# Three edits in a two-model chain of local-attention layers: where the root's steps lie, how far ahead one model projects, and the loop order of a product

## The chip, the cores and the metric

The kernel runs on one core of a Trainium2 chip. The core has five engines that run side by side, each through its own list of instructions in order: TensorE (PE; its weight loads are listed as PEld), VectorE (DVE), ScalarE (ACT), GpSimd (POOL) and SyncE (SP), which here issues the DMAs. They wait for one another through semaphores. Matrix products land in PSUM, which PE writes and DVE and ACT read; the tiles of all other data lie in SBUF. The metric is the device time of one execution in microseconds (us), lower is better.

## The reference, cut to what matters

Two models follow each other on an input of shape (2, 2048, 128). Each is modulated, attends, and then runs a chain of local-attention layers:

- first model: an attention stage, then 6 layers with 16 heads of 64, windows of 32
- second model: a linear-attention stage, then 2 layers with 8 heads of 64, windows of 64

The part that the change touches is inside the local-attention layers. For each layer:

```
def l2norm(t):
    return t / jnp.clip(jnp.linalg.norm(t, axis=-1, keepdims=True), 1e-12)
...
q, k, v = jnp.split(h @ wqkv, 3, axis=-1)
q = l2norm(q) * qs
k = l2norm(k) * ksc
q, k = rotary_xpos(q, k)
o = local_attention(q, k, v)     # softmax over the window before and the own window
x = x + o @ wo
h = layernorm(shift_token(x)) @ w1 + b1
x = x + (a * gelu(g)) @ w2 + b2  # a, g: the halves of h
```

Everything is float32. The root of the title is the reciprocal square root of the sum of squares of every head of queries and keys, that is, l2norm.

## The kernel before, in words

The first model's attention stage runs up to about 600 us of the span and is not touched. Then `local_models` runs all 8 layers as one list of 256 tiles: layer by layer, 16 tiles of 128 tokens for each of the 2 sequences, the two sequences taking turns. Tiles 0 to 191 are the first model's, 192 to 255 the second's.

A loop over rounds i (L1461) works on several tiles at once. In round i:

- `scores(i + 1)`: on PE a mask (L986) and the products of queries and keys (L995) into a wide buffer; DVE takes the maximum (L1003) and subtracts it (L1005). Then ACT takes the exponential (L1012), DVE sums (L1019) and inverts (L1020), and POOL multiplies (L1021).
- `project(i + 3, ...)`, once for each unit of the model (the first model has two units, for its 2048 columns of queries and keys, the second has one): two products (L871) into a wide buffer `pq`; ACT squares it (L873); DVE multiplies it by the cosine table into `r` (L881) and, with the halves swapped, by the sine table into `t2` (L886); POOL adds the two (L892). After the last unit DVE sums the squares of each head (L897), takes the root in `rsqrt_quick` (L167 to L180, nine small instructions), and POOL multiplies `r` by it (L904).
- `keys_first_(i)`: the weights of tile i are transposed (L1030) and copied by ACT (L1031).
- `mix(i)`: the value product (L1048), copied by ACT (L1054).
- `values(i + 2)`: the value projection (L955), copied by ACT (L956) and spread to windows by SP's DMAs (L963 to L968).
- `turn(i + 2, u)`: `r` is transposed (L936) and copied to query and key tiles by ACT (L939, L941). Tile i + 2 was projected in round i - 1.
- `project_out(i)`: the output product (L1065), added to the residual by DVE (L1071).

Between these calls a round takes two steps (`step`) from a list of feed-forward work and up to six (`lstep`) from a list of the second model's linear-attention work. `feed_forward` adds seven steps after every fourth tile of a sequence: centring (L1096), variance (L1105, L1108, L1110), a pause, scaling (L1128, L1131), two times three products (L1148) with ACT (L1158) or DVE (L1165) behind, and a last product (L1173, L1179). The linear-attention steps run while the first model's last layer ends and the second's first layer starts. A tile of the second model whose input isn't complete forces further steps (`while (b, t // 4) not in ready`).

PSUM has eight banks of 512 float32 in each partition. `wide` gives out two buffers of two banks (pool `f_psA`) and `bank` four buffers of one bank (pool `f_psT`):

```
psA = ctx2.enter_context(tc.tile_pool(name="f_psA", bufs=2, space=PSUM))
psT = ctx2.enter_context(tc.tile_pool(name="f_psT", bufs=4, space=PSUM))
```

The scores and the projections take wide buffers, and so do some of the linear-attention steps; all other products take single banks. In the kernel before, L897 and the root's steps write into `pq`, the wide buffer of the last unit, once the product in it has been used:

```
y = rsqrt_quick([pq[:, k * 32:k * 32 + 2 * H] for k in range(4)], 2 * H, wk)
```

A wide buffer is free when the last reader of what it holds is done. The first model takes three of them in a round (scores, unit 0, unit 1), so the next round's unit 0 gets the buffer of this round's unit 1.

The framework (tile pools) inserts the waits, and it plans the order of the instructions of each engine from the traced program, its own estimate of durations and the buffers that are free then. So the order on an engine is near that of the source, but not the same: in the trace the first records of a value product (L1048) often stand ahead of a value projection (L955), and the rest of the product behind it.

In `mix` the value product is cut into many small products. For the first model each works on 64 of the 128 rows (the key group s) and 64 of the 128 columns (the half q): four quarters of PE's array, each with weights of 64 x 64 and 32 columns of data. The second model has one key group (NO is 1), so each takes all rows and one half of the columns. Every float32 product stands in the trace as two records.

## Time and profile before

| | us |
|---|---|
| median of 3 runs (4983.2 to 4993.75) | 4991.75 |
| the profiled execution | 4992.08 |
| its span (first to last instruction) | 4990.3 |
| PE busy in the span | 4522.4 |
| DVE busy | 3949.9 |
| POOL busy | 2783.4 |
| ACT busy | 2641.9 |

The profile is that of one execution. Its page gives busy time of each engine and the busy share in 40 slices of the span, each of them 125 us. Groups of instructions are named by line, engine, operation and tile names (written <- read). A row of the waits names the instruction that an idle engine was waiting to start and what it waited for; a PE wait is time that PE is idle. PEclk is the clock that PE was granted, 1.00 being full speed. In the timeline each row has the start in us from the span's start, the length in us, the engine, the line, what was done and how often (x), and in square brackets the idle time of the engine before it. PE's matmuls overlap each other, so the length of a group of them includes the tail of the last one.

The stages that the text speaks of: the first model's layers from 600 to 3700 us, the change of models with its linear attention from 3700 to 4300, the rest of the second model from 4300 on.

### The profile page before, as it was taken

What the parts mean: (1) busy time and instruction counts of PE and PEld (TensorE: products, weight loads), DVE (VectorE), ACT (ScalarE), POOL (GpSimd) and SP (SyncE); (2) the same over time, 40 slices, a digit from 0 to 9 for tenths busy, and PEclk for the clock granted to TensorE, in tenths of its full rate; (3) what the DMA queues carried; (4) which work ended last, traced back from release to release, by engine and by line L of the source; (5) the groups of instructions that cost most, each with busy time, mean ns of one, the idle gap of its engine ahead of it and who ended that gap; (6) DMA issues with size and microseconds to landing.
All of it is one profiled execution on the core that took longest, in us unless ns stands there. A gap on an engine that the chain in (4) does not pass through costs nothing.

```text
span 4990.3 us, 166474 instructions
## 1 busy us (share of the span) xinstructions
PE 4522.4 (91%) x73028; PEld 3080.9 (62%) x73058; DVE 3949.9 (79%) x6840; ACT 2641.9 (53%) x4207; POOL 2783.4 (56%) x1666
## 2 busy tenths in 40 slices
PE   5667799999999999999999999999999998989887
PEld 3445566666666666666666666666666665555554
DVE  6993488888887888888888888888877777778776
ACT  3223355555555555555555555555555555555554
POOL 3332366666666666666666666666555544455552
PEclk8778899999999999999999999999999999999999
DMA  2000222223222322232222322232221211111111
GB/s 77 1 1 25 84 68 67 64 72 78 68 64 63 84 71 64 64 82 72 65 70 61 80 67 64 66 82 68 55 58 49 63 45 40 40 46 40 50 48 41
DMA packets 222468, 295.32 MB, mean 59 GB/s; under 512 B 75656, under 2 KB 95408, under 8 KB 221744
## 3 DMA queue, kind: packets, MB, share of 16 engines
q1 hardware_dynamic: 221744, 284.67, 22.1%
q8 instruction: 576, 9.44, 0.8%
q14 instruction: 148, 1.21, 0.1%
HBM read 40.98 MB, written 10.75 MB: 10 GB/s over the span
## 4 chain that ended last, share of the span: by engine, by line
PE 47%; DVE 25%; ACT 7%; POOL 6%; issue 4%; DMA 1%; SPq 0%; POOLq 0%; DVEq 0%; ACTq 0%
PE ps_qk L871 11%; PE ps_o L1048 5%; PE ps_f L1148 5%; DVE ps_qk L897 5%; PE ps_v L955 5%; DVE t L886 5%; PE ps_turn L936 4%; POOL r L892 4%; PE ps_y L1065 4%; PE ps_s L995 3%; DVE r L881 3%; PE ps_fy L1173 3%; DVE rs L1019 2%; ACT sq L873 2%; PE ps_pT L1030 2%
## 5 line engine op out<-in xcount | busy, mean ns | idle before, releaser
L892 POOL TENSOR_TENSOR r<-r,t 128x1024 f32<-128x1024 f32 x448 | 1061.8, 2370 | 926.2 <-DVE t L886 814.6
L904 POOL TENSOR_TENSOR r<-r,rq_y 128x1024 f32<-128x1024 f32 x448 | 844.5, 1903 | 521.8 <-DVE rq_y L180 498.9
L873 ACT ACTIVATE sq<-ps_qk 128x1024 f32<-128x1024 f32 x448 | 461.0, 1029 | 1091.5 <-PE ps_qk L871 1026.4
L871 PE MATMUL ps_qk<-wp,hs 128*128 128x512 f32 x1792 | 894.9, 622 | 110.0 <-DVE rq_y L180 82.6
L881 DVE TENSOR_TENSOR r<-ps_qk,tb 128x1024 f32<-128x1024 f32 (+1 forms) x512 | 550.9, 1076 | 215.2 <-ACT sq L873 200.9
L1048 PEld LDWEIGHTS ps_o<-pT,v 64*64 64x64 f32 (+1 forms) x26624 | 479.4, 136 | 309.5 <-ACT pT L1031 162.4
L886 DVE TENSOR_TENSOR t<-ps_qk,tb 128x1024 f32<-128x1024 f32 (+1 forms) x512 | 554.5, 1083 | 145.5 <-POOL r L892 145.0
L1021 POOL TENSOR_TENSOR sm<-sm,rs 128x1024 f32<-128x1024 f32 x256 | 487.9, 1906 | 255.5 <-DVE rs L1020 172.7
L1048 PE MATMUL ps_o<-pT,v 64*64 64x32 f32 (+1 forms) x26624 | 532.1, 221 | 36.5 <-ACT pT L1031 19.9
L897 DVE TENSOR_REDUCE ps_qk<-sq 128x16 f32<-128x1024 f32 x448 | 549.2, 1226 | 12.0
L871 PEld LDWEIGHTS ps_qk<-wp,hs 128*128 128x128 f32 x1792 | 310.5, 193 | 367.6 <-issue 236.5
L936 PEld LDWEIGHTS ps_turn<-ident,r 128*128 128x128 f32 x3584 | 413.1, 144 | 157.0 <-issue 98.2
L936 PE MATMUL ps_turn<-ident,r 128*128 128x128 f32 x3584 | 450.1, 278 | 40.4 <-POOL r L904 36.9
L955 PE MATMUL ps_v<-wp,hs 128*128 128x512 f32 x896 | 482.2, 640 | 1.1 <-ACT oT L1054 0.8
L1065 PEld LDWEIGHTS ps_y<-oT,wo 128*128 128x128 f32 x3584 | 432.1, 193 | 48.3 <-issue 43.0
L1065 PE MATMUL ps_y<-oT,wo 128*128 128x128 f32 x3584 | 448.5, 277 | 1.7 <-ACT oT L1054 1.5
L1003 DVE TENSOR_REDUCE mx<-ps_s 128x16 f32<-128x1024 f32 (+1 forms) x256 | 312.5, 1221 | 101.5 <-PE ps_s L995 99.6
L1054 ACT COPY oT<-ps_o 128x512 f32<-128x512 f32 x448 | 243.8, 588 | 276.0 <-PE ps_o L1048 275.2
L995 PE MATMUL ps_s<-kT,qT 64*32 64x64 f32 (+1 forms) x26624 | 384.1, 231 | 0.3 <-issue 0.3
L995 PEld LDWEIGHTS ps_s<-kT,qT 64*32 64x32 f32 (+1 forms) x26624 | 331.0, 108 | 63.1 <-issue 49.4
L1148 PE MATMUL ps_f<-fx,w 128*128 128x512 f32 (+1 forms) x768 | 364.5, 612 | 2.3 <-DVE fx L1131 1.9
L1019 DVE TENSOR_REDUCE rs<-sm 128x16 f32<-128x1024 f32 (+1 forms) x256 | 310.6, 1213 | 62.3 <-ACT sm L1012 61.2
(265 smaller groups left out, 6860.3 us busy)
## 6 DMA issues: line engine op xcount, KB each, us to landing
v<-vn SPq DMA_DIRECT2D x1276, 128.0 KB
v<-vn SPq DMA_DIRECT2D x744, 64.0 KB
v<-vn SPq DMA_DIRECT2D x64, 256.0 KB
wp<-in_L_ffn_Wqkv SPq DMA_DIRECT2D x20, 512.0 KB
xD<-xb SPq DMA_DIRECT2D x24, 256.0 KB
xb<-xD SPq DMA_DIRECT2D x24, 256.0 KB
cs<-in_cos SPq DMA_DIRECT2D x128, 32.0 KB
cs<-in_sin SPq DMA_DIRECT2D x128, 32.0 KB
```

Of the source, the lines that this page charges most:

```text
L871: nc.tensor.matmul(pq[:, js], lhsT=hw, rhs=wts[g, u][:, js], start=True, stop=True)
L881: nc.vector.tensor_tensor(r[:, es].rearrange("p (h d) -> p h d", d=DH), pq[:, es].rearrange("p (h d) -> p h d", d=DH), bc(tb[:, 0, s].unsq ...
L886: nc.vector.tensor_tensor(t2[:, es].rearrange("p (h s d) -> p h s d", s=2, d=32), pq[:, es].rearrange("p (h s d) -> p h s d", s=2, d=32)[: ...
L892: nc.gpsimd.tensor_tensor(r, r, t2, ALU.add)
L897: nc.vector.tensor_reduce(pq[:, 16 * v:16 * v + 16], st[i].pop(("sq", v)).rearrange("p (h d) -> p h d", d=DH), AX.X, ALU.add,)
L904: nc.gpsimd.tensor_tensor(rv, rv, bc(y[:, 16 * v:16 * v + 16].unsqueeze(2), (128, 16, DH)), ALU.mult)
L936: nc.tensor.transpose(p[:, c * 128:(c + 1) * 128], r[:, cs], ident)
L955: nc.tensor.matmul(p, lhsT=hw, rhs=wv, start=True, stop=True)
L995: nc.tensor.matmul(sp[W * w:W * w + W, c0:c0 + 2 * W], lhsT=qT[64 * q:64 * q + 64, cc, W * w:W * w + W], rhs=kT[64 * q:64 * q + 64, cc, W ...
L1048: nc.tensor.matmul(po[s][64 * q:64 * q + 64, 128 * c + W * w:128 * c + W * w + W], lhsT=v2[kp, w, co:co + 64], rhs=pT[kp, q, c, W * w:W * ...
L1065: nc.tensor.matmul(py[:, 0:128], lhsT=wts[g, "o"][:, c * NO + s, :], rhs=oT[:, s, c, :], start=(c + s == 0), stop=(c == 3 and s == NO - 1),)
L1148: nc.tensor.matmul(ps_[c][0:sz], lhsT=wts[g, "w1"][:, o:o + sz], rhs=S["x"], start=True, stop=True,)
```

## The change

It has three parts. First, L897 and the root's steps write into a single bank `ss` of the pool of four, instead of into the wide buffer `pq`. Second, a tile of the second model is projected four rounds ahead instead of three: a table `rounds` says which tiles are projected in a round, and since tile 191 is projected in round 188 and tile 192 too, that round has both. The second model's `r` takes turns between the two tags that the first model has for its two units, so that it has four buffers. Third, in `mix` the loop over the key group s (row halves) becomes the outer and the loop over q (column halves) the inner one of the two.

```diff
-            r = wk.tile([128, 1024], F32, name=f"r{u}", bufs=2)
+            r = wk.tile(
+                [128, 1024], F32, tag=f"r{u if len(units) == 2 else i % 2}", name="r", bufs=2
+            )
...
+                ss = bank("ss")
                 for v in range(len(units)):
                     nc.vector.tensor_reduce(
-                        pq[:, 16 * v:16 * v + 16],
+                        ss[:, 16 * v:16 * v + 16],
                         st[i].pop(("sq", v)).rearrange("p (h d) -> p h d", d=DH), AX.X, ALU.add,
                     )
-                y = rsqrt_quick([pq[:, k * 32:k * 32 + 2 * H] for k in range(4)], 2 * H, wk)
+                y = rsqrt_quick([ss[:, k * 32:k * 32 + 2 * H] for k in range(4)], 2 * H, wk)
...
                 for w in range(m.NW):
-                    for q in range(2):
-                        co = 128 * c + 64 * q
-                        for s in range(NO):
-                            kp = slice(2 * W * s, 2 * W * (s + 1))
+                    for s in range(NO):
+                        kp = slice(2 * W * s, 2 * W * (s + 1))
+                        for q in range(2):
+                            co = 128 * c + 64 * q
                             nc.tensor.matmul(
...
+        rounds = {}
+        for j in range(n):
+            rounds.setdefault(j - (3 if len(layers[tiles[j][0]][0].units) == 2 else 4), []).append(j)
         for i in range(-3, n):
-            j = i + 3
             lstep()
...
-            more = False
-            if j < n:
+            for j in rounds.get(i, ()):
                 g, b, t = tiles[j]
...
-                lstep()
+            lstep()
             step()
...
-            if j < n:
+            for j in rounds.get(i, ()):
+                g, b, t = tiles[j]
+                jj = j % per
+                nu = len(layers[g][0].units)
+                more = g < last
                 project(j, nu - 1)
```

## The prediction, made before the change was run

> **What bounds the kernel now.** I read the busy shares first, then the same shares by stage, then TensorE's waits in each stage, and last one wait in the timeline. All sums are made against the profiled execution: 4992.1 us, of which its span is 4990.3 and 1.8 lies around it. The median of the runs shown is 4991.75, so both stand for the same time. A measurement of this kernel can tell about 0.2% (10 us) from no change.

> The page, engines over the whole span and in 40 slices:
> ```profile
> PE 4522.4 (91%) x73028; PEld 3080.9 (62%) x73058; DVE 3949.9 (79%) x6840; ACT 2641.9 (53%) x4207; POOL 2783.4 (56%) x1666
> ...
> PE   5667799999999999999999999999999998989887
> ...
> DVE  6993488888887888888888888888877777778776
> ```
> TensorE (PE) is busy 9 tenths or more from slice 7 on; VectorE (DVE) never is. By stage (first model, change of models, second model; the columns are the stretch, its length, busy PE, PEld, DVE, ACT, POOL, then the granted PE clock):
> ```profile
> 600.00:3700.00 3100.00, 2977.08 (x56700) 2048.85 (x56700) 2583.03 (x4180) 1769.10 (x2778) 1986.25 (x1156) 0.99 0.28 69
> 3700.00:4300.00 600.00, 556.42 (x6820) 372.74 (x6820) 446.92 (x870) 329.02 (x501) 294.73 (x192) 0.96 0.18 49
> 4300.00:4990.30 690.30, 594.69 (x5113) 377.37 (x5108) 516.72 (x1077) 350.28 (x527) 321.40 (x200) 0.94 0.16 45
> ```
> PE is 96% busy in the first model and DVE 83%: PE sets the pace, and only PE's own idle time (123 us there) and its clock can be won. In the second model PE is 86% busy and idle 96 us. What ends those idle times, first stage and then last stage (waiter, releaser: us in all, times, longest):
> ```profile
> PE ps_qk L871 <- DVE rq_y L180: 82.3, 80, 3.7
> PE ps_o L1048 <- issue: 14.4, 19, 1.8
> PE ps_qk L871 <- DVE sm L1005: 8.8, 16, 3.4
> ```
> ```profile
> PE ps_turn L936 <- POOL r L904: 32.8, 11, 3.5
> PE ps_out L1439 <- DVE xb L1195: 13.2, 4, 4.6
> PE ps_o L1048 <- ACT pT L1031: 10.0, 28, 0.7
> PE ps_r L1128 <- POOL frt L1110: 6.6, 2, 4.3
> PE ps_qk L871 <- DVE sm L1005: 6.0, 11, 0.8
> PE ps_s L986 <- DVE rq_y L180: 5.0, 5, 2.0
> ```
> The first line is the wide buffer. The last unit's product holds it until the root's last step (L180); the second wide buffer after it is the next round's first product (L871). One such wait:
> ```profile
> 2525.84 1.23 DVE L886 TENSOR_TENSOR t<-ps_qk,tb 128x1024 f32<-128x1024 f32 x1 [1.30 <-POOL r L892]
> ...
> 2533.28 0.19 DVE L180 SCALAR_TENSOR_TENSOR rq_y<-ps_qk,rq_g 128x32 f32<-128x32 f32 x1
> ...
> 2533.53 3.05 PE L871 MATMUL ps_qk<-wp,hs 128*128 128x512 f32 x4 [1.84 <-DVE rq_y L180]
> ```
> The last reader that needs the product itself, L886, ended at 2527.07, before PE went idle at 2531.7. And the product then took 3.05 us, where undisturbed ones take 1.98: the clock fell.
> ```profile
> 2531.60:2533.50 1.90, 0.09 (x4) 0.00 (x0) 1.70 (x11) 0.00 (x0) 0.00 (x0) 1.00 0.24 73
> 2533.50:2536.90 3.40, 3.37 (x7) 1.58 (x8) 2.33 (x2) 0.28 (x1) 3.28 (x2) 0.62 0.00 0
> 4697.00:4705.00 8.00, 5.64 (x13) 3.31 (x14) 4.17 (x13) 3.87 (x6) 7.31 (x6) 0.58 0.22 64
> ```
> The clock records of 600 to 3700 hold 16 stretches at half clock, 61 us; 12 of them, 48 us, begin within 8 us of such an L871 wait. From 4300 on there are 82 us at half clock; 58 us begin at one of the L936 waits (the third line is one).

> **Part 1, root in its own bank.** Removed: the hold of the wide buffer by L897 and the nine root steps, so 82.3 us of waits go. What is late next is the second product of the round, which needs the buffer of the scores, freed by L1005. I went through the 80 waits one by one: the smaller of the wait and of the time by which the second product started after L1005's end adds up to 62 us. That is kept; the other 20 us become waits on L1005. Half clock costs half of a stretch: 48 us of it are 24 us at most; I take two thirds, 16. In the last stage the 5.0 us of L986 on L180 go too: 5.

> [...]

> Added: one more tenant of the four single banks, per round. Its DVE instructions are the same as before, on another address of PSUM, so they cost nothing new (L897 1226 ns, each step about 0.19 us). New are two waits. L897 must wait for a free bank; behind it on DVE stand the root, the residual L1071, then the scores' L1003; POOL's L904 waits for the root. And PE's tenants (transposes L936, L1065, pT, value products) have three banks while the root holds one: 4.8 us of a round of 15 (2511.86 to 2516.68) in the first model, 7.3 (4688.39 to 4695.66) in the second. At the tightest, 2512.4 to 2513.7, two transposes, the output product and the root's bank make four: it just fits. The trace has no such wait to read: the present PE waits for a bank that ACT empties are a few us in all. Bounds: nothing, or one ACT copy (L939, 596 ns) in each of 256 rounds, 150 us. The nearest row is the present few us, so I take a sixth, 0.1 us a round: 26. It could not gain by itself.

> **Part 2, second model projected four tiles ahead.** Removed: L936 waits for r from POOL's L904, 32.8 us in 11 waits. The rounds there last about 13.7 us (the waits at 4699 and 4809 stand eight rounds apart) and the longest wait is 3.5, so a round more covers them all; late next is the transposed weights' copy (L1031, at most 0.7 us each). I keep 30. Half clock after them: 58 us, so 29 at most; I take 18. Moved with it: per tile one product (1.98 us of PE), Square, four multiplications, the POOL add and multiplication, the tables' two DMAs and POOL multiplications. Their number doesn't change. Four r buffers instead of two come from tags that the first model already has. The other engines' tiles keep their buffers. The step of the linear layers' list is made once a round as before, and by counting the calls no forced step is needed (the last two blocks are ready in rounds 205 and 210 and asked for in 212 and 213). Once, round 188 projects two tiles (1.98 us of PE more, and the first table of the second model is asked for in the round that uses it, its DMAs included): 5 us, bounds 2 to 15. At the end one round has no projection: that product has only moved to round 188.

> **Part 3, order of the value product.** Only the first model's order changes (with one key group the two loops are the same). The number of instructions stays. Rows (start, length, then the count at the end of the line):
> ```profile
> 2522.14 2.15 PE L1048 MATMUL ps_o<-pT,v 64*64 64x32 f32 x128
> ...
> 394.34 1.87 PE L530 MATMUL ps_r<-vt,wt 64*64 64x64 f32 x58 [0.78 <-ACT wt L502]
> ```
> Less the last record's 0.22 us, the first is 15.2 ns a record over four quarter arrays, 61 ns per quarter; L530, whose neighbours share rows and alternate columns, is 28.9 ns over two quarters, 58 ns per quarter. So a quarter sets its own pace and neighbours of the same rows run side by side: nothing. Bounds: L530's 28.9 ns for all 128 records, 1.75 us a round, 192 rounds: +337 us; the scores' row (L995, 64*32, about 10.7 ns from start to start) would be -4.5 ns: -110 us. I take 0, by the per-quarter pace, which both rows share.

> [...]

> **Sum.** 62 + 16 + 5 + 30 + 18 = 131 won; 26 + 5 = 31 lost; 100 us in all: 4992 - 100 = 4892 us.

> **Rivals.**
> Full gain: no new wait, 82 + 24 + 5 + 33 + 29 = 173: 4819. For it: PE at 96% with nothing else late. Against: DVE is 83% busy and late in exactly the waiting rounds. 14%.
> Absorbed: the change doesn't free what it says, since L873 and L886 still hold the product and L1005 the scores; the waits go over to them, and of the clock half is won: 4992 - 17 + 5 = 4980, bounds 4970 to 5000. For it: the 8.8 us on L1005 exist already. Against: L886 ends long before the waits. 11%.
> Slower, the bank: the output product L1065 (starts 2512.73) lands in the bank that the root frees at 2516.68 and PE waits 3.95 us. In one of four of the first model's 192 rounds that is 190 us in place of the 26: 4992 - 131 + 5 + 190 = 5056. It decides from one round in six on (126 / 3.95 = 32 rounds). For it: four banks for twelve tenants a round. Against: a bank that is free sooner can be taken, and the order of the engines was planned with the banks. 13%.
> Slower, the order: 4892 + 337 = 5229. 4%.
> The forecast, with its own range 4850 to 4950: 58%.

> Faster by over 0.2%: 58 + 14 + 3 of the absorbed case = 75%. Within: 8%. Slower: 13 + 4 = 17%. The range, 4815 to 5010, takes in the full gain and the absorbed case with their bounds; left out are the order's case, most of the bank's and the edges, some 2 in 10.

> **What would show it.** L871's wait on L180 gone, one on L886 or L1005 in its place (under 25 us); L936's wait on L904 gone after 4300; PE clock of both stages up by about 0.01 and 0.03; L1048 at 15 ns a record. Wrong if L897, L936, L1065 or L955 wait for banks by over 130 us in all, or if a mix takes over 2.5 us.

## The result: 14.6% slower

The changed kernel takes 5713.3 us (median of 4 runs) against 4987.5 us of the kernel before on the same chip: a ratio of 1.1464, interval 1.1433 to 1.1496. The forecast was 4892, the range ended at 5010. The profiled execution has a span of 5711.9 us, 721.6 more than before.

Behind the edited lines the numbers have moved by two or three: L888 is the old L886, L900 the old L897, L907 the old L904, L939 the transposes of the turn (L936), L958 the value projection (L955), L989 and L998 the scores' mask and products, L1051 the value product (L1048), L1068 the output product (L1065) and L1074 its residual (L1071). In kernels of the experiments they differ by one or two again; the tile names say which is which.

The page of the changed kernel, engines over the span and in 40 slices (now 143 us each):
```profile
PE 4741.0 (83%) x73028; PEld 3230.1 (57%) x73058; DVE 3979.4 (70%) x6840; ACT 2667.8 (47%) x4217; POOL 2776.2 (49%) x1666
...
PE   5667788888898888888888888888899888877777
...
DVE  6972676777677776777777776777777666766665
```
PE, 9 tenths busy or more before, is at 8; DVE fell with it. Nothing was put in place of PE as the bound: both engines wait, and for each other. PE's idle time in the span went from 467.9 to 970.9 us (+503.0), its busy time from 4522.4 to 4741.0 (+218.6) for the same instructions; the two make the 721.6.

The same three stretches as before (length, busy PE, PEld, DVE, ACT, POOL, then the granted PE clock):
```profile
600.00:3700.00 3100.00, 2682.89 (x48743) 1830.95 (x48744) 2212.84 (x3568) 1518.84 (x2371) 1702.89 (x988) 0.94 0.24 59
3700.00:4300.00 600.00, 532.70 (x9020) 364.17 (x9019) 427.89 (x709) 300.31 (x467) 319.08 (x191) 0.95 0.23 58
4300.00:5711.90 1411.90, 1128.01 (x10876) 749.12 (x10874) 937.26 (x1859) 657.66 (x980) 576.95 (x371) 0.90 0.15 40
```
The first model no longer ends near 3700, so 600 to 3700 lies wholly in it: PE 87% busy (96% before) and DVE 71% (83%), at a clock of 0.94 instead of 0.99. The busy time grew because of the clock (the sum stands further down, with the account of the prediction).

What ends PE's idle time, whole span, the lines that count (waiter, releaser: us in all, times, longest):
```profile
PE ps_turn L939 <- DVE rq_y L180: 272.0, 106, 5.6
PE ps_s L989 <- DVE t L888: 179.8, 108, 2.6
PE ps_y L1068 <- DVE rq_y L180: 64.7, 16, 4.4
...
PE ps_f L1151 <- DVE rq_y L180: 28.6, 10, 4.0
...
PE ps_r L1131 <- DVE rq_y L180: 17.9, 5, 4.1
PE ps_fy L1176 <- DVE rq_y L180: 17.9, 6, 3.3
...
PE ps_qk L871 <- DVE t L888: 13.3, 6, 3.2
PE ps_v L958 <- DVE rq_y L180: 11.7, 3, 6.5
PE ps_c L1099 <- DVE rq_y L180: 10.8, 5, 3.3
```
The first product L871 doesn't wait for the root (L180) any more, as part 1 meant. But nearly every tenant of the four single banks now does: the seven lines shown that end in L180 add up to 423.6 us in 151 waits, where before L871 and the mask waited 88.3 us for it. The turn heads the list. It needs nothing of that root: it transposes an `r` that was finished a round ago. It waits for the bank. The trace names no banks; that it is the bank follows from what the turn reads and from the own pool below (e6, e11), with which this wait is gone.

DVE's waits show the other half. The first line is of before, the second of the changed kernel:
```profile
DVE hs L1071 <- PE ps_y L1065: 92.0, 83, 5.3
```
```profile
DVE hs L1074 <- PE ps_y L1068: 489.8, 195, 8.5
```
One round of the changed kernel in the timeline, PE and then DVE:
```profile
2404.90 0.39 PE L989 MATMUL ps_s<-L_maskb,pick 64*128 64x512 bf16 x2 [1.93 <-DVE t L888]
2405.22 2.72 PE L1051 MATMUL ps_o<-pT,v 64*64 64x32 f32 x128
2407.87 2.91 PE L958 MATMUL ps_v<-wp,hs 128*128 128x512 f32 x4
2410.62 1.04 PE L939 MATMUL ps_turn<-ident,r 128*128 128x128 f32 x8
2413.09 1.06 PE L939 MATMUL ps_turn<-ident,r 128*128 128x128 f32 x8 [1.44 <-DVE rq_y L180]
...
2414.43 1.95 PE L1068 MATMUL ps_y<-oT,wo 128*128 128x128 f32 x16
```
```profile
2408.52 2.48 DVE L900 TENSOR_REDUCE ps_ss<-sq 128x16 f32<-128x1024 f32 x2
...
2412.76 0.19 DVE L180 SCALAR_TENSOR_TENSOR rq_y<-ps_ss,rq_g 128x32 f32<-128x32 f32 x1
...
2416.42 0.59 DVE L1074 TENSOR_TENSOR hs<-ps_y,hs 64x128 f32<-64x128 f32 x2 [1.10 <-PE ps_y L1068]
```
The root holds its bank from 2408.52 to 2412.95. The first half of the turn finds banks, the second half starts 0.14 us after the root has ended. The output product stands behind the turn on PE, so it is late too, and DVE, done with the root, idles until it comes. PE waits for DVE and then DVE for PE. That isn't so in every round: the kernel has 256 roots, PE waits for 151 of them in the lines above, and DVE waits for the output product 195 times.

### The profile page after: what moved, and what is told of

Read it like the earlier page. It is cut to its first block, busy times and chain, and to the rows that moved or that the text cites. A ratio compares the mean times of both kernels' runs of the same rounds, so it can differ in the third digit from the quotient of the medians.

```text
span 5711.9 us, 166280 instructions
## 1 busy us (share of the span) xinstructions
PE 4741.0 (83%) x73028; PEld 3230.1 (57%) x73058; DVE 3979.4 (70%) x6840; ACT 2667.8 (47%) x4217; POOL 2776.2 (49%) x1666
## 3 DMA queue, kind: packets, MB, share of 16 engines
q1 hardware_dynamic: 221744, 284.67, 19.2%
## 4 chain that ended last, share of the span: by engine, by line
PE 45%; DVE 31%; ACT 7%; POOL 4%; issue 3%; DMA 0%; POOLq 0%; DVEq 0%; ACTq 0%; SPq 0%
PE ps_y L1068 7%; PE ps_qk L871 7%; DVE t L888 6%; PE ps_s L998 6%; PE ps_turn L939 5%; DVE ps_ss L900 5%; DVE r L883 5%; PE ps_f L1151 4%; PE ps_v L958 4%; PE ps_o L1051 4%; DVE rs L1022 4%; POOL r L894 3%; PE ps_fy L1176 3%; ACT sq L873 2%; DVE mx L1006 2%
## 5 line engine op out<-in xcount | busy, mean ns | idle before, releaser
L907 POOL TENSOR_TENSOR r<-r,rq_y 128x1024 f32<-128x1024 f32 x448 | 843.9, 1902 | 212.1 <-DVE rq_y L180 208.3
L873 ACT ACTIVATE sq<-ps_qk 128x1024 f32<-128x1024 f32 x448 | 460.6, 1028 | 985.6 <-PE ps_qk L871 931.6
L871 PE MATMUL ps_qk<-wp,hs 128*128 128x512 f32 x1792 | 878.2, 611 | 20.8 <-DVE t L888 13.3
L939 PE MATMUL ps_turn<-ident,r 128*128 128x128 f32 x3584 | 494.7, 287 | 275.6 <-DVE rq_y L180 272.0
L939 PEld LDWEIGHTS ps_turn<-ident,r 128*128 128x128 f32 x3584 | 436.3, 149 | 457.1 <-issue 240.8
L888 DVE TENSOR_TENSOR t<-ps_qk,tb 128x1024 f32<-128x1024 f32 (+1 forms) x512 | 553.3, 1081 | 145.4 <-POOL r L894 145.3
L1051 PE MATMUL ps_o<-pT,v 64*64 64x32 f32 (+1 forms) x26624 | 538.2, 227 | 70.0 <-issue 39.3
L1051 PEld LDWEIGHTS ps_o<-pT,v 64*64 64x64 f32 (+1 forms) x26624 | 494.9, 143 | 150.9 <-issue 99.1
L958 PE MATMUL ps_v<-wp,hs 128*128 128x512 f32 x896 | 553.5, 741 | 17.3 <-DVE rq_y L180 11.7
L1068 PE MATMUL ps_y<-oT,wo 128*128 128x128 f32 x3584 | 498.4, 296 | 66.1 <-DVE rq_y L180 64.7
L900 DVE TENSOR_REDUCE ps_ss<-sq 128x16 f32<-128x1024 f32 x448 | 546.1, 1219 | 8.6 <-ACT g L1389 2.3
L1068 PEld LDWEIGHTS ps_y<-oT,wo 128*128 128x128 f32 x3584 | 479.5, 211 | 119.5 <-DVE rq_y L180 68.5
L1074 DVE TENSOR_TENSOR hs<-ps_y,hs 64x128 f32<-64x128 f32 x512 | 147.9, 289 | 494.9 <-PE ps_y L1068 489.8
L1006 DVE TENSOR_REDUCE mx<-ps_s 128x16 f32<-128x1024 f32 (+1 forms) x256 | 313.5, 1225 | 206.2 <-PE ps_s L998 204.9
L871 PEld LDWEIGHTS ps_qk<-wp,hs 128*128 128x128 f32 x1792 | 306.5, 191 | 263.7 <-issue 228.7
L998 PE MATMUL ps_s<-kT,qT 64*32 64x64 f32 (+1 forms) x26624 | 391.2, 234 | 2.2 <-issue 1.2
L944 ACT COPY kT<-ps_turn 128x512 f32<-128x512 f32 x448 | 250.2, 604 | 268.1 <-PE ps_turn L939 267.8
```

The costliest lines, as they stand in the source:

```text
L871: nc.tensor.matmul(pq[:, js], lhsT=hw, rhs=wts[g, u][:, js], start=True, stop=True)
L888: nc.vector.tensor_tensor(t2[:, es].rearrange("p (h s d) -> p h s d", s=2, d=32), pq[:, es].rearrange("p (h s d) -> p h s d", s=2, d=32)[: ...
L900: nc.vector.tensor_reduce(ss[:, 16 * v:16 * v + 16], st[i].pop(("sq", v)).rearrange("p (h d) -> p h d", d=DH), AX.X, ALU.add,)
L907: nc.gpsimd.tensor_tensor(rv, rv, bc(y[:, 16 * v:16 * v + 16].unsqueeze(2), (128, 16, DH)), ALU.mult)
L939: nc.tensor.transpose(p[:, c * 128:(c + 1) * 128], r[:, cs], ident)
L958: nc.tensor.matmul(p, lhsT=hw, rhs=wv, start=True, stop=True)
```

## The experiments

The theories that the expectations name. A: the root's tenancy of one of the four banks. B: another part, or parts that hurt each other. C: the wide buffer that comes free early, which lets the planner put the scores' mask ahead of the value product, where it waits (the 179.8 us above). D, later: three banks are simply too few for the rest. Each ratio is against the kernel before on the same chip.

**Each part alone, and the root without a bank.** e1 is part 1 alone, e2 part 2 alone, e3 part 3 alone, each with its part of the diff above. e4 frees the wide buffer but takes no bank:
```diff
+                ss = wk.tile([128, 128], F32, name="ss", bufs=1)   # e4, instead of bank("ss")
-            cs = wk.tile([128, 2, DH], F32, name="cs", bufs=2)
+            cs = wk.tile([128, 2, DH], F32, name="cs", bufs=1)
```
e1, expected:

> Part 1 alone: L897 and the root's steps in a single bank, everything else as before. Theory A (the bank: the root holds one of four single banks, so transposes, output products and feed-forward products wait for its last step): nearly the whole loss is here, 5600 to 5760 us. Theory B (the loss comes from the other parts, the loop order or the projection ahead): at most 5100 us. Theory C (not the bank, but the wide buffer that is free early: the mask of the next scores is put ahead of the value product and PE waits for L886 there): also 5600 to 5760 us, so this run doesn't tell C from A.

Measured: 5746.9 us, ratio 1.1525 (1.1472 to 1.1579). The whole loss is in part 1. Its waits are those of the changed kernel:
```profile
PE ps_turn L937 <- DVE rq_y L180: 320.9, 124, 5.6
PE ps_s L987 <- DVE t L886: 179.2, 108, 2.8
PE ps_y L1066 <- DVE rq_y L180: 60.2, 15, 4.4
```
e2, expected:

> Part 2 alone: the second model's tiles projected four rounds ahead, the root in the wide buffer and the old loop order. Theories A and C: the transposes no longer wait for POOL's r, 4930 to 4975 us. Theory B: 5050 us or more.

Measured: 4935.6 us, 0.9892 (0.9873 to 0.991). The turn's wait for POOL went from 36.9 us (whole span) to 3.5, the half clock after 4300 from 82 to 45 us. This is the fastest version of the study, and it beats both kernels.

e3, expected:

> Part 3 alone: column halves alternate first in the value product. Theories A and C, and the quarter-array reading of the trace: 4980 to 5000 us, 15 ns from record to record as before. Theory B (neighbours of the same rows can't run side by side): up to 5320 us.

Measured: 5010.9 us, 1.0038 (1.0019 to 1.0057): a small loss. Start to start at full clock, where no idle time lies between them, the records of the first model's value product follow each other every 15.2 ns before and every 15.4 ns here.

e4, expected:

> Part 1 in another way: L897 and the root's steps in a small SBUF tile, so that the wide buffer is free as early as in part 1 but no single bank is taken (the tables' load buffer goes from two to one to make room). Theory A: the waits of the first product on the root go and nothing takes their place, 4890 to 4960 us. Theory C: the early free wide buffer brings the mask forward and the loss with it, 5300 us or more.

Measured: 4985.8 us, 0.9992 (0.998 to 1.0005). That an early wide buffer alone costs hundreds of microseconds is refuted. But the gain is missing too: the wait on L180 went over to L1005 (L1006 here), 19.2 before,
```profile
PE ps_qk L871 <- DVE sm L1006: 63.4, 58, 3.4
```
and DVE is busy 165 us longer (4115.1 us against 3949.9), for which the root's first step is enough: it takes 827 ns instead of 192 on average, 163 us for 256 roots.

**How many banks, and whose.** e5 is the kernel before with `bufs=3` for the single banks and the root in the wide buffer; e6 is part 1 with the root's bank in a pool of its own, three banks for the rest:
```diff
-        psT = ctx2.enter_context(tc.tile_pool(name="f_psT", bufs=4, space=PSUM))
+        psT = ctx2.enter_context(tc.tile_pool(name="f_psT", bufs=3, space=PSUM))     # e5, e6
+        psR = ctx2.enter_context(tc.tile_pool(name="f_psR", bufs=1, space=PSUM))     # e6
...
+                ss = psR.tile([128, 512], F32, tag="R", name="ss")                   # e6
```
e5, expected:

> The kernel before with three single banks in place of four, and the root left in the projection's buffer as before: no root tenancy at all. Theory D (the count: three banks for the work of four are too few, and the first part loses because it takes one away most of the time): slower by most of the 754 us that the first part lost alone, 5400 to 5750. Theory A (the order of tenancy: the root's sums hold one bank for the 4.43 us from the first reduce to L180's end, and the work queued behind on TensorE needs just that one): a small loss, 4990 to 5150. Theory C (the loss is the planner's other order, which puts the scores' mask matmul early): not changed unless the order changes, about 4990.

Measured: 5074.5 us, 1.0157 (1.0132 to 1.0182). One bank fewer costs 82 us, not 754: D falls. In the profile PE idles 18 us longer and is busy 64 us longer, at the same granted clock (0.956); what stretches its products stays open. The wait for the wide buffer is still there (L871 on L180: 65.2 us, 82.6 before).

e6, expected:

> The first part alone, but the root's bank comes out of a pool of its own with one buffer, and the other pool keeps three banks: eight banks in all, as before. Theory A: the turn, the output product and the feed-forward no longer wait for L180; between 4900 and 5150, no more than 2 per cent from the kernel with three banks. Theory D: as slow as the kernel with three banks, both at or above 5400. Theory C: the projection's buffer still comes free early, so the planner again puts the mask early: 5150 to 5350 with about 180 us of waits of the mask on t L886.

Measured: 4994.0 us, 1.0008 (0.9989 to 1.0027). A root that has a bank to itself costs none of the 754 us, although the rest has only three. Not one PE wait ends at L180. Against e5, with the same three banks, freeing the wide buffer is worth 80.5 us.

e7 is the changed kernel with the scores' mask matmul behind the products, so that it can't be put ahead of them:
```diff
-                    start=True, stop=False,                  # mask
+                    start=False, stop=True,
...
-                        start=False, stop=(cc == HPG - 1),   # products, now first
+                        start=(cc == 0), stop=False,
```

> The changed kernel with one edit: in the scores the mask's matmul comes after the 64 products of its half and ends the accumulation, where it began it before, so the mask can't be put ahead of the products. If the 180 us that the mask waited for t L888 are a cause of their own (C): 5480 to 5580. If they are only where PE's wait shows itself, PE being held by the same chain anyway (A): the wait goes to the first product or the next instruction in line, 5650 to 5760.

Measured: 6090.8 us, 1.2189 (1.2162 to 1.2215), still slower. Without the early mask the turn waits for the root by itself, 4.7 us each time:
```profile
PE ps_turn L939 <- DVE rq_y L180: 653.0, 139, 8.3
```
So the early mask is not what makes the changed kernel slow, and C falls: without it PE waits longer, and at the turn. That it would be 380 us slower was foreseen by neither theory; against the changed kernel PE idles 260 us longer and is busy 111 us longer, of which half clock makes 92 (1032.9 us busy at half clock against 849.9).

e8 is the changed kernel with the root in SBUF, as in e4:

> The changed kernel with all three parts, but the root's scratch is a tile in SBUF and not a bank. If the bank is the whole of the loss (A and D): what the parts gave one by one, 4992.6 - 6.8 (SBUF scratch) - 57.0 (queries and keys further ahead) + 18.4 (order) = 4947, within 4925 to 4970. If the parts also hurt each other (B): above 5000.

Measured: 5005.4 us, 1.0022 (1.0009 to 1.0035). The loss is gone, but 58 us of the sum are missing. DVE is busy for 4114.7 us, as in e4.

**The parts together, without the shared bank.** e9 is parts 1 and 2 with the root's own bank, e10 parts 2 and 3 without part 1, e11 the changed kernel with the root's own bank.

> Parts 1 and 2, with the root's bank in a pool of its own (three banks are left to the rest). If the gain of the tile further ahead (57 us alone) does not touch the root's place: 4994 - 57 = 4937, within 4920 to 4955. If both gains come from the same waits (the turn on POOL r stood at 50.9 us with the root's own bank), or three banks press harder with the turn moved: 4975 to 5010.

Measured: 4956.7 us, 0.9926 (0.9905 to 0.9948), just above what was expected.

> Parts 2 and 3 without part 1: the root stays in the projection's buffer. If the two parts only add: 4992.6 - 57.0 + 18.4 = 4954, within 4940 to 4968. If they hurt each other, and this is why the changed kernel with the root in SBUF took 5005 in place of 4947: 4985 to 5015.

Measured: 4951.9 us, 0.9915 (0.9891 to 0.9939). The two parts add up; B falls for them, and what e8 misses comes only with the root in SBUF.

> The changed kernel with all three parts, the root's bank in a pool of its own and three for the rest. If the bank's place in the rotation is all that the 720 us come from: within 30 us of the sum of the parts, 4994 - 57 + 18 = 4955, so 4925 to 4985. If the parts also hurt each other: 4990 to 5040.

Measured: 4968.1 us, 0.9954 (0.9937 to 0.997). The changed kernel loses 745 us for one thing, the pool that the root's bank comes from. The round that stands at the same place in e11, PE and then DVE:
```profile
2403.40 2.26 PE L1052 MATMUL ps_o<-pT,v 64*64 64x32 f32 x128
2405.58 1.98 PE L959 MATMUL ps_v<-wp,hs 128*128 128x512 f32 x4
2407.40 2.00 PE L940 MATMUL ps_turn<-ident,r 128*128 128x128 f32 x16
2409.24 2.04 PE L1069 MATMUL ps_y<-oT,wo 128*128 128x128 f32 x16
```
```profile
2409.96 1.22 DVE L901 TENSOR_REDUCE ss<-sq 128x16 f32<-128x1024 f32 x1
...
2413.01 0.17 DVE L180 SCALAR_TENSOR_TENSOR rq_y<-ss,rq_g 128x32 f32<-128x32 f32 x1
2413.22 0.29 DVE L1075 TENSOR_TENSOR hs<-ps_y,hs 64x128 f32<-64x128 f32 x1
```
The order is that of the changed kernel, but for the mask and one feed-forward step (L1131): value product, value projection, turn, output product. This is no single case: between 600 and 3600 us that is the commonest order on PE in all three kernels. The mask stands ahead of the value product in the changed kernel (117 of 150 sequences from one tile's scores to the next), behind the output product in e11 (93 of 189) and behind the scores in e7 (106 of 137). So e7 and e11 have PE's order in common but for the mask at the scores, and only e7, with the shared pool, has the turn's waits on L180. In e11 the turn runs through while the root is under way, the output product ends at 2411.28, before the root does, and DVE goes from the root's steps to the residual without a pause.

**A shorter hold.** In e12, part 1 alone, the reduces write to SBUF and the bank is taken for the root's steps only; e13 is the same with the bank from a pool of its own:
```diff
+                sums = wk.tile([128, 32], F32, name="sums", bufs=2)
-                        pq[:, 16 * v:16 * v + 16],
+                        sums[:, 16 * v:16 * v + 16],
...
+                ss = bank("ss")                                       # e13: psR.tile(...)
+                y = rsqrt_quick([sums[:, 0:2 * H]] + [ss[:, k * 32:k * 32 + 2 * H] for k in range(1, 4)], 2 * H, wk)
```
(`cs` has one buffer here too.)

> Part 1 alone, but the two reduces write to SBUF and the root takes one of the four banks only for its eight steps, about 1.6 us of the 4.43. Theory A by length (each us of the hold is a us in which the next tenant waits): the 754 us fall to about a third, 5150 to 5350. Theory A by place (the bank comes free only at L180, the last step, however short the hold was, and what stands behind it in the rotation waits for that): hardly better than the first part alone, 5600 to 5750. If a short tenancy finds a free bank without putting anything behind it: 4970 to 5020.

Measured: 6523.4 us, 1.3069 (1.3029 to 1.3108): outside all three. The wait is another one:
```profile
PE ps_qk L871 <- DVE t L886: 987.2, 234, 7.3
```
In most rounds of its timeline the next tile's first product stands ahead of this tile's value product, and it waits for a wide buffer that DVE empties. So this kernel has another order and says nothing of what a shorter hold is worth.

> As the short hold (the reduces write to SBUF, a bank only for the root's steps), but that bank comes from a pool of its own and three are left to the rest. If the 1530 us of the short hold come from the root's tenancy in the shared pool, which moves the plan so that the next tile's product stands ahead of the value product and waits for t L886: these waits (987 us) go, 4980 to 5080. If they come from the reduces in SBUF, whichever bank the steps use: again above 6000.

Measured: 4982.1 us, 0.999 (0.9976 to 1.0003); the 987 us are gone. Again it is the tenancy in the shared pool, this time by the order that was planned with it.

## Why the prediction was wrong

| term of the sum | predicted, us | measured, us | from |
|---|---|---|---|
| part 1: wide buffer, its clock, L986 | -83 | -80.5 | e6 against e5 |
| part 1: one bank fewer for the rest | +26 | +81.5 | e5 against before |
| part 1: the tenancy in the shared pool | in the 26 | +753, +745 | e1 against e6, changed against e11 |
| part 2 | -43 | -57 | e2 against before |
| part 3 | 0 | +18, +16 | e3 against before, e10 against e2 |

With the first number of each line the sum is +715 us; the changed kernel is 726 slower. The two runs of a line can be of different chips; the kernel before took 4987 to 4993 us on each.

**The step that failed** is "Added" of part 1: "one more tenant of the four single banks", bounded by one ACT copy a round, 150 us, and taken as "0.1 us a round: 26". Both the value and the bound were wrong, for two reasons. The price was read from waits for banks that ACT empties in 0.6 us, but the new tenant is emptied by DVE after 4.43 us of reduces and root (2408.52 to 2412.95). And the fit ("it just fits") was tried on the timeline of before, though the order and the banks are planned anew with the change. What the runs show in its place: the second half of the turn gets the bank that the root is in. That ties a tile's turn to the root of the next tile, two things that had nothing to do with each other. The waits that the prediction named as the sign of being wrong came: the turn, the output product and the value projection wait 348 us for the bank, over the 130 that it allowed. The turn stands ahead of the output product on PE, the residual and the scores' maximum stand behind the root on DVE, and so the two engines take turns (e11 against the changed kernel shows the round with and without the tie).

The timeline shows how dear such a tie is: the output product of the changed kernel started at 2414.43, behind a turn that waited 1.44 us, until 2413.09, and in e11 it followed, at 2409.24, on a turn that didn't wait.

**The price of the wait alone would not have been enough.** Of the 503 us of additional PE idle time the waits on L180 are 335 (423.6 - 88.3). Nearly 180 are the mask on L888; in e7, where the mask can't wait there, the turn waits longer instead (653.0 us against 272.0). The 219 us of additional busy time are the clock: half clock held for 358 us of 600 to 3700 and 276 us after 4300, against 61 and 82, and half of the 491 us more is 246. Counted over the whole span, and only where PE was busy, half clock held for 849.9 us against 366.8; half of the difference is 242.

**The rival "slower, the bank"** had the kind of mechanism, a PE product in the bank that the root frees, and its price: the output product's 16 waits cost 64.7 us, 4.0 each, as foreseen with 3.95. It had the place and the number wrong. The main waiter is the turn, and the waits on L180 are 151, not 48; what DVE, the mask and the clock add was not in it. So it gave 5056, with 13%.

**What was right.** L871's wait on L180 is gone, and what is left on L888 and L1008 is under 25 us (13.3 and 6.6). The worth of the wide buffer was right within 3 us where the bank doesn't disturb it. That it is so close is luck: each of the two times is known to about 10 us, and the 20 us that were to go over to L1005 didn't (24.6 us in e5, 25.8 in e6), while the turn's wait on POOL rose from 31.7 to 50.9. And the same 80 us are lost by giving the rest three banks, so that part 1 can't gain even with a bank of its own (e6). Part 2 kept what was predicted: 33.4 us of the turn's waits (predicted 30) and 37 us less at half clock, 19 us (predicted 18); the remaining few us are within what can be measured. Part 3's pace per quarter held nearly: 15.4 ns a record for 15.2, which makes 4 us of its loss of 18. In the profile, of e3's slowest run (8 us above its median), PE is busy 22 us longer (4544.2 against 4522.4), and 13 of these are the clock (392.8 us busy at half clock against 366.8). The starts of value products that waited for nothing visible rose from 14.6 to 26.9 us. The cause of that isn't settled.

**The rival "slower, the order"** didn't come: with every second neighbour in the same rows the records go from 15.2 to 15.4 ns, not to the 28.9 of L530, and the kernel with part 3 alone is nowhere near 5229 (e3, 5010.9).

**Two readings of the prediction** were inexact, and neither bears on the miss. PE is not at 9 tenths in all slices from the seventh on: slices 34, 36, 38 and 39 are at 8 and the last at 7. The twelve half-clock stretches include one of 6.8 us behind a wait of 3.43 us on L1005 (at 3583.31), so that 41 us of half clock follow the 80 waits on L180, not 48: 14 us in place of 16.

**Open.** Why the planner gives the turn that bank, and why it puts the next product early in e12, depends on its own estimates, which no trace shows. What a shorter hold is worth in an unchanged order wasn't seen. Why e7's turn waits so much longer than the changed kernel's, what the 82 us of a missing bank consist of, and where the 58 us lie that e8 lacks against the sum of its parts, is open.

## What to carry to other kernels

A buffer taken from a shared pool can't be priced by its own hold alone: the same root cost nothing measurable in a bank of its own (e6). What counts is who gets the buffer next and what is queued behind that one: ask which engine frees it, after what chain, and whether the next tenant had anything to do with that chain before. A short test tells it apart: the same edit with a buffer in a pool of its own, and the old kernel with one buffer less (here +1 and +82 us, against +754 with the pool shared). And where a framework plans the order, the old timeline does not show which tenants will meet.

## What the runs showed of the hardware

In e4 the first two of the root's DVE steps were much dearer in SBUF than in PSUM: 827 and 335 ns on average, 192 and 185 in the kernel before. The first, 128 x 32 elements, took 171 ns (median of 12) where POOL was idle all through and 682 ns (of 91) where it worked all through, the second 182 and 379. In PSUM, in the kernel before, the first took 199 ns with POOL idle and with POOL at work, the second 191 and 191.
